# The preparation of the first scan segment, moved from behind the two opening fronts into the plan that holds them

## The chip, the cores and the metric

The kernel runs on one core of a Trainium2 chip, in one launch. The metric is the device time in microseconds (us). The engines named below are PE (matrix engine), DVE (vector), ACT (activations), POOL and SP; SP issues nearly all DMAs, in the order of its own queue. Every engine works its instructions off in program order, so the order in which the program is written out decides what can run beside what.

## The reference, cut to what matters

The input is a batch of 4 images of 64 x 64 tokens with 96 channels. Four layers follow one another. Layers 0 and 1 are state space layers: group norm, an input projection to 192 channels plus a gate z, a 3 x 3 depthwise convolution with SiLU, then a recurrence over the 4096 tokens in four directions, each with a state of 16 per channel:

```
h = h * exp(dt * A) + (dt * u) * B_t        # per channel and state
y = sum over states of h * C_t
```

`dt`, `B` and `C` are projections of the convolved tokens, taken in the order of the direction (in layer 0 two diagonal orders and two radial ones). The four results are summed in token order, normed, gated with z and projected. Layers 2 and 3 (attention, a Fourier mixer and feed-forward parts) come after the scans and are not touched here.

## The kernel before

`Stream.run` handles eight batches, four images for each of the two scan layers. Each batch has 4 directions of 4 segments of 1024 tokens, so 128 segments. Every batch passes three stages.

- **Front** (`front`, L348): four strips of 16 image rows are loaded (`measure` L368 the strip into a tile `da`, `edges` L380 its neighbour rows `halo`). DVE takes statistics (L372, L388), two tiny matmuls average them over groups (L391, L400), ACT takes the square root (L66). Then each strip is projected (`project`: L428 and L434 for x, L444, L447 and the store L452 for the gate) and convolved on PE (`convolve`: L481 the taps, L493 SiLU, L502 and L505 back to token rows, L514 the store to `x_tok` in DRAM).
- **Preparation** of a segment (`fetch` L736, `prepare` L779). The tokens are gathered from `x_tok` in scan order: for a diagonal direction one small DMA for each diagonal run (L745), 52 of them for the first segment. PE transposes them (L791), ACT puts them in order (L804), PE projects (L830), ACT and POOL form a softplus (L834, L835, L839, L818 to L822, L856), PE adds its three terms (L862), ACT copies `dt` (L867), POOL multiplies `dt` by x (L866, L876). B and C go to DRAM (L841), `dt` too (L869). They come back broadcast over partitions: B and C by `load_states` (L883, eight DMAs of 512 KB), `dt` by `load_dt` (L889).
- **Scan**: for 6 channel blocks and 4 state groups, PE spreads u (L898), ACT takes `exp` of the decays (L906), DVE multiplies by B (L911) and scans (L918), POOL multiplies by C (L928), PE sums over states (L939). In the middle of the kernel a segment's preparation is woven into the scan of the segment before it.

The fronts are put out by `side_by_side` (L686). It makes generators, called threads, and a `Plan` writes them out in the order of an estimated start on their engine: a thread yields an engine and a guess of the time, or a condition to wait for. Tiles in a `Rings` are marked taken and free while the program is written; a front that wants the PSUM bank `m` (one buffer) waits until its flag is free. Where the plan finds PE unoccupied it writes small spare matmuls (`fill`, L705).

The first call of `side_by_side` puts out the fronts of the first two batches; the second of them starts when every strip of the first is projected (`first.to_project == 0`). After that call, `run` writes the first segment's preparation alone, one step after the other, and then its eight B and C loads and the first `dt` load:

```python
self.side_by_side(batches[:2])
self.fetch(segs[0])
self.run_hooks(len(self.hooks), len(self.runs))
weave.start(self.prepare(segs[0]))
weave.finish()
```

`prepare` also counts in `self.put` how much PE time it has put out; `keep_busy` (L955) writes spare matmuls (L962) into the scan while that count is low.

Of the kernel before, what the change touches and what calls it, by code (L numbers as in the profile page):

```python
# [21 lines left out]
B = 4  # L22
HW = 64
L = HW * HW
# [4 lines left out]
SEG = 1024  # L29
# [8 lines left out]
NSG = NS // GS  # L38
# [162 lines left out]
class Rings:  # L201
# [9 lines left out]
    def take(self, pool, shape, tag, bufs, dtype=F32):  # L211
        ring = self.rings.setdefault(tag, SimpleNamespace(busy=[False] * bufs, at=0, tiles=None))
        while ring.busy[ring.at]:
            yield lambda: not ring.busy[ring.at]
        slot, ring.at = ring.at, (ring.at + 1) % bufs
        ring.busy[slot] = True
        x = ring.tiles[slot] if ring.tiles else self.k.t(pool, shape, tag, dtype, bufs=bufs)
        self.slots[id(x)] = ring, slot, x
        return x

    def give(self, *xs):
        for x in xs:
            ring, slot, _ = self.slots.pop(id(x))
            ring.busy[slot] = False
# [87 lines left out]
class Stream:  # L312
# [38 lines left out]
    def front(self, bt, plan, rings, first=None):  # L351

        k, nc, lay = self.k, self.nc, bt.lay
        take, give = rings.take, rings.give
        if first:
            yield lambda: first.to_project == 0
        bt.to_project = L // SEG
        x = lay.x_in[:, bt.b, :]
        bt.x_tok = k.t(self.dram, [L, DI], "x_tok", bufs=3)
        bt.z_t = k.t(self.dram, [C, 2, L], "z_t", bufs=3)  # L360
# [104 lines left out]
        def convolve(s, st):  # L465
            yield lambda: st.pad is not None
            xc = []
            for _ in range(C // GC):
                xc.append((yield from take(self.tmp, [128, CH], "xc", 3)))

            two = yield from take(self.ps_t, [128, 2, CH], "t", 2)
            one = yield from take(self.ps, [128, CH], "m", 1)
            ps = [two[:, 0, :], two[:, 1, :], one]
            yield "PE", 8.0
            for tap in range(9):
                dy, dx = divmod(tap, 3)
                for blk in range(C // GC):
                    mine = slice(blk * GC, (blk + 1) * GC)
                    for at in range(4):
                        half, j = divmod(at, 2)  # L480
                        nc.tensor.matmul(  # L481
                            ps[blk][at * GC : (at + 1) * GC, :],
                            lay.diag[mine, half, tap, :],
                            st.pad[mine, half, j * 8 + dy : j * 8 + dy + 8, dx : dx + HW],
                            start=tap == 0,
                            stop=tap == 8,
                            tile_position=(blk * GC, at * GC),
                        )
            give(st.whole)
            del st.whole, st.pad  # L490
            for blk in range(C // GC):
                yield "ACT", 0.7
                nc.scalar.activation(xc[blk], ps[blk], AF.Silu, bias=lay.conv_b[:, blk : blk + 1])  # L493
            give(two, one)
            del two, one, ps
            rows = yield from take(self.tmp, [128, 2, 4, DI], "y_rows", 1)
            two = yield from take(self.ps_t, [128, 2, CH], "t", 2)
            one = yield from take(self.ps, [128, CH], "m", 1)
            for blk, ps in enumerate((two[:, 0, :], two[:, 1, :], one)):
                yield "PE", 1.2  # L500
                for t in range(4):
                    nc.tensor.transpose(ps[:, t * 128 : (t + 1) * 128], xc[blk][:, t::4], k.ident)  # L502
                yield "ACT", 0.8
                for half in range(2):
                    nc.scalar.copy(  # L505
                        rows[:, :, :, half * C + blk * GC : half * C + (blk + 1) * GC],
                        ps.rearrange("p (t h j d) -> p h j t d", h=2, j=2, d=GC)[:, half],
                    )
            give(two, one, *xc)
            del two, one, ps, xc  # L510

            to = bt.x_tok[s * SEG : (s + 1) * SEG, :].rearrange("(j p t) d -> p j (t d)", j=2, t=4)
            yield "SP", 0.1
            nc.sync.dma_start(to, rows.rearrange("p j t d -> p j (t d)"))  # L514
            yield "none", 2.5
            give(rows)
            del rows

        works = [work for s, st in enumerate(strips) for work in (project(s, st), convolve(s, st))]
        yield from plan.together(works)  # L520

# [164 lines left out]
    def side_by_side(self, ahead, behind=None, flush=None, seg=None):  # L686


        k, nc = self.k, self.nc
        plan, rings = Plan(), Rings(k)  # L690
        self.ended, self.idle = False, None

        def ending():

            yield "none", 1.2
            if flush:
                flush()
            self.idle = k.t(self.ps_y, [128, CH], "y")
            self.ended = True
            yield "PE", 4.0  # L700

        def fill():
            if self.idle is not None:
                data = self.layers[0].diag.rearrange("p h t c -> p (h t c)")[:, :384]
                nc.tensor.matmul(self.idle[:GC, :384], self.zeros, data, start=True, stop=True)  # L705

        def states():

            for at in range(2 * NSG):
                yield "none", 50.0 if at == 0 else 4.0  # L710
                yield "SP", 0.1
                self.load_states(seg, *divmod(at, NSG))
            self.load_dt(seg, 0)

        plan.fill = fill
        if seg:
            plan.add(states())
        if behind:
            plan.add(self.merge(behind, plan, rings))
        for bt in ahead:  # L720
            plan.add(self.front(bt, plan, rings, None if bt is ahead[0] else ahead[0]), 1)
        plan.add(ending())
        plan.run()
        self.idle = None
# [11 lines left out]
    def fetch(self, seg):  # L736
# [11 lines left out]
        if seg.bt.lay.ordered and seg.kd < 2:  # L748

            for j in range(SEG // 128):  # L750
                at = seg.i * SEG + j * 128
                seg.turned[j] = []
                for pos, n, token, step in diagonal_runs(seg.kd, at, at + 128):
                    self.runs.append(lambda to=g[pos - at : pos - at + n, j, :], r=(token, n, step): run(to, *r))
                    seg.turned[j].append((pos - at, n, step < 0))
        elif seg.bt.lay.ordered:
            for j in range(SEG // 128):
                at = seg.i * (SEG // 128) + j
                self.hooks.append(
                    lambda j=j, at=at: nc.gpsimd.indirect_dma_start(  # L760
                        out=g[:, j, :],
                        out_offset=None,
                        in_=x_tok,
                        in_offset=bass.IndirectOffsetOnAxis(ap=self.order[:, seg.kd, at : at + 1], axis=0),
                    )
                )
        elif seg.kd % 2 == 0:
            at = self.start(seg)
            nc.sync.dma_start(g, x_tok[at : at + SEG, :].rearrange("(j p) d -> p j d", p=128))
        else:  # L770
            for w in range(2):
                nc.sync.dma_start(g[w * HW : (w + 1) * HW], self.by_columns(x_tok, seg, w))
# [238 lines left out]
    def run(self):  # L1011
# [1 line left out]


        k, nc, weave = self.k, self.nc, self.weave
        batches = [SimpleNamespace(lay=lay, b=b, to_project=1) for lay in self.layers for b in range(B)]
        segs = []
        for bt in batches:
            for kd in range(ND):
# [5 lines left out]
        slots = [(seg, cb, sg) for seg in segs for cb in range(NCB) for sg in range(0, NSG, 2)]  # L1025
        first_of = lambda slot: (slot[0].kd, slot[0].i, slot[1], slot[2]) == (0, 0, 0, 0)
        with k.tc.manual_schedule():
            self.side_by_side(batches[:2])
            self.fetch(segs[0])
            self.run_hooks(len(self.hooks), len(self.runs))  # L1030
            weave.start(self.prepare(segs[0]))
            weave.finish()
            for which in range(2):
                for sg in range(NSG):
                    self.load_states(segs[0], which, sg)
            self.load_dt(segs[0], 0)
            now, before = [], []

            def flush():
# [1071 lines left out]
```

## Time and profile before

| | us |
|---|---|
| median of 3 runs | 15879.18 |
| lowest and highest of the 3 runs | 15832.05 and 15962.23 |
| the profiled execution's own time | 15861.73 |
| its span in the profile | 15859.9 |
| first scan instruction (L918) starts at | 400.95 |
| last decay of the scans (L906) starts at | 12645.2 |

Over the whole span PE is busy 86%, DVE 81%, ACT 52% and POOL 62%; the mean granted PE clock of the execution is 0.875. Times inside the profile count from the start of the span. A row of a timeline gives start and duration, the engine, the line, the operation and its tiles, how many instructions are merged in it, and in brackets how long the engine was idle ahead of it and what ended that. SPq is SP's queue: its rows are the issuing of DMAs, not their transfer.

### The profile page before, as it was taken

To read this page: it belongs to the slowest core of one execution; us is meant where nothing else is said; L and a number is where in the kernel's file an instruction comes from. 1 tells how busy PE (TensorE), PEld (TensorE's weight loads), DVE (VectorE), ACT (ScalarE), POOL (GpSimd) and SP (SyncE) were. 2 spreads that over 40 slices of the span, in tenths; PEclk is the share of its full clock that TensorE was granted. 3 is DMA by queue.
4 is the path that set the end of the run, shared out by engine and by line. 5 is a ranking of instruction groups with operands and counts; after the bars stand their busy time and mean duration, and the time that the engine had idled before them with its cause. 6 is when DMAs were issued, how large, how long until landed. Compare 5 with 4: busy or idle time off the path is not lost. (4 is left out here: it accounts for less than half of the span.)

```text
span 15859.9 us, 190275 instructions
## 1 busy us (share of the span) xinstructions
PE 13616.6 (86%) x70721; PEld 4897.8 (31%) x70721; DVE 12867.0 (81%) x9642; ACT 8291.1 (52%) x14188; POOL 9781.6 (62%) x4913
## 2 busy tenths in 40 slices
PE   7888888888888888888888888888888889998877
PEld 3222322232223222322222223222222234443344
DVE  1989798979897989799979997999899965665555
ACT  3656465556565655556655655656556522332333
POOL 0788688867886788677757775777677730000223
PEclk8888888888898888888888888888888899998888
DMA  2333433343334333433343334333433310000132
GB/s 71 110 103 121 153 108 104 120 152 106 104 122 153 106 103 120 154 109 115 113 150 118 108 118 147 111 122 116 141 118 108 115 53 18 18 11 14 46 75 70
DMA packets 662747, 1637.10 MB, mean 103 GB/s; under 512 B 102822, under 2 KB 268459, under 8 KB 658044
## 3 DMA queue, kind: packets, MB, share of 16 engines
q1 hardware_dynamic: 624956, 1549.37, 30.9%
q0 software_dynamic: 36864, 75.55, 1.6%
q8 instruction: 560, 9.18, 0.2%
q14 instruction: 367, 3.01, 0.1%
HBM read 1295.03 MB, written 329.58 MB: 102 GB/s over the span
## 5 line engine op out<-in xcount | busy, mean ns | idle before, releaser
L928 POOL TENSOR_TENSOR hc<-h,bc 128x1024 f32<-128x1024 f32 x3072 | 7186.7, 2359 | 2360.7 <-DVE h L918 1949.8
L918 DVE TENSOR_TENSOR_SCAN h<-da,state,t 128x1024 f32<-128x1024 f32 x2304 | 5271.5, 2329 | 11.5 <-ACT da L906 8.7
L939 PE MATMUL y<-hc,gather_y 128*32 128x512 f32 x12288 | 4270.8, 687 | 628.4 <-POOL hc L928 465.1
L911 DVE TENSOR_TENSOR t<-u,bc 128x1024 f32<-128x1024 f32 x3072 | 3601.2, 1218 | 895.2 <-PE u L898 780.8
L906 ACT ACTIVATE da<-dts,L_A_logs 128x1024 f32<-128x1024 f32 x3072 | 3488.0, 1147 | 726.7 <-DMA dts<-dt_dram 444.4
L898 PE MATMUL u<-dtu,spread 32*128 32x512 f32 x3072 | 1879.7, 739 | 369.4 <-DVE t L911 362.9
L962 PE MATMUL y<-L_diag,zeros 96*32 96x256 f32 x5218 | 1736.9, 463 | 0.0
L918 DVE TENSOR_TENSOR_SCAN h<-da,t 128x1024 f32<-128x1024 f32 x768 | 1711.0, 2269 | 13.1 <-ACT da L906 12.5
L939 PEld LDWEIGHTS y<-hc,gather_y 128*32 128x32 f32 x12288 | 800.1, 117 | 2404.0 <-issue 1210.4
L830 PE MATMUL m<-xs,proj 96*128 96x512 f32 (+1 forms) x2048 | 1018.3, 620 | 121.8 <-ACT dt L839 62.7
L867 ACT COPY dt<-m 96x512 f32<-96x512 f32 x512 | 297.1, 580 | 1458.9 <-PE m L862 1458.9
L898 PEld LDWEIGHTS u<-dtu,spread 32*128 32x128 f32 x3072 | 595.1, 214 | 1433.1 <-issue 1117.5
L962 PEld LDWEIGHTS y<-L_diag,zeros 96*32 96x32 f32 x5218 | 617.2, 132 | 1274.9 <-issue 1114.7
L1289 POOL MEMSET padp<- 128x2448 f32 x32 | 68.6, 2143 | 1396.7 <-PE d L1329 1375.5
L1365 DVE SCALAR_TENSOR_TENSOR hcv<-padv,taps,hcv 128x2048 f32<-128x2048 f32 x384 | 902.2, 2350 | 13.4
L1329 PE MATMUL d<-padp,diag 32*32 32x512 f32 x25600 | 885.5, 601 | 2.0 <-ACT hcp L1344 2.0
L822 POOL TENSOR_TENSOR dtu<-sp_z,dtu 96x1024 f32<-96x1024 f32 x256 | 604.4, 2361 | 384.7 <-ACT dtu L820 382.3
L862 PE MATMUL m<-sp_z,ident 96*96 96x512 f32 x1024 | 537.1, 606 | 195.6 <-ACT sp_z L856 195.6
L834 ACT ACTIVATE sp_z<-m,L_dtb 96x512 f32<-96x512 f32 x512 | 349.3, 682 | 540.4 <-PE m L830 531.6
L1329 PEld LDWEIGHTS d<-padp,diag 32*32 32x32 f32 x25600 | 483.4, 103 | 370.6 <-issue 197.7
L986 ACT COPY spare<-m 128x512 f32<-128x512 f32 x384 | 225.6, 587 | 711.0 <-PE m L983 710.8
L830 PEld LDWEIGHTS m<-xs,proj 96*128 96x128 f32 (+1 forms) x2048 | 322.4, 177 | 829.4 <-issue 325.8
(275 smaller groups left out, 15623.6 us busy)
## 6 DMA issues: line engine op xcount, KB each, us to landing
bc<-bc_dram SPq DMA_DIRECT2D x1024, 512.0 KB
dts<-dt_dram SPq DMA_DIRECT2D x768, 512.0 KB
dt_dram<-dt SPq DMA_DIRECT2D x256, 384.0 KB
y_tok<-spare SPq DMA_DIRECT2D x64, 768.0 KB
dt<-y_tok SPq DMA_DIRECT2D x128, 384.0 KB
x_tok<-y_rows SPq DMA_DIRECT2D x32, 768.0 KB
z_t<-z_rows SPq DMA_DIRECT2D x64, 384.0 KB
dx<-x_tok SPq DMA_DIRECT2D x64, 384.0 KB
```

Of the source, the lines that this page charges most:

```text
L822: rest = lambda half: nc.gpsimd.tensor_add(r[:, half], z[:, half], r[:, half])
L830: nc.tensor.matmul(ps, proj[:, src, to], xs[:, src, cols], start=src == 0, stop=src == 1)
L862: nc.tensor.matmul(ps, k.ident[:C, :C], term[:, half, cols], start=at == 0, stop=at == 2)
L898: self.nc.tensor.matmul(seg.u[:, cols], self.spread[rows, :], seg.dtu[rows, half, cols], start=True, stop=True)
L906: self.nc.scalar.activation(da, seg.dts[cb], AF.Exp, scale=seg.bt.lay.neg_a[:, seg.kd, g : g + 1])
L911: self.nc.vector.tensor_mul(gr.t, gr.seg.u, self.bc[:, 0, gr.sg, :])
L918: self.nc.vector.tensor_tensor_scan(gr.h[:, order], gr.da[:, order], gr.t[:, order], start, op0=ALU.mult, op1=ALU.add)
L928: self.nc.gpsimd.tensor_mul(gr.hc, gr.h, self.bc[:, 1, gr.sg, :])
L939: nc.tensor.matmul(seg.y[at : at + GC, :], self.gather_y, gr.hc[:, part * CH : (part + 1) * CH], start=gr.sg == 0, stop=gr.sg == NSG - 1, ...
L962: self.nc.tensor.matmul(gr.seg.y[at : at + GC, :256], self.zeros, gr.seg.bt.lay.diag.rearrange("p h t c -> p (h t c)")[:, :256], start=Fal ...
L1329: nc.tensor.matmul(pc[i][j * 32 : (j + 1) * 32, :], diag[mine, ON_PE.index(t), tap, :], pad[mine, j * 8 + dy : j * 8 + dy + 8, dx : dx + H ...
L1365: nc.vector.scalar_tensor_tensor(to, win, wt, to, op0=ALU.mult, op1=ALU.add)
```

## The change

A thread `begin` joins the first call of `side_by_side`. It waits until the first batch has put out all its four stores of `x_tok` (the new counter `to_store`), writes the gathers, then steps through `prepare`, and at the end writes the eight loads of B and C and the first load of `dt`. While it steps it marks the bank `m` as taken. Afterwards it sets `self.put` to zero. The serial block in `run` goes.

```diff
-        bt.to_project = L // SEG
+        bt.to_project = bt.to_store = L // SEG
...
             nc.sync.dma_start(to, rows.rearrange("p j t d -> p j (t d)"))
+            bt.to_store -= 1
...
+        def begin(rings):
+
+            yield lambda: ahead[0].to_store == 0
+            self.fetch(seg)
+            self.run_hooks(len(self.hooks), len(self.runs))
+            yield "none", 6.0
+            work = self.prepare(seg)
+            bank = rings.rings["m"].busy
+            going = True
+            while going:
+                while bank[0]:
+                    yield lambda: not bank[0]
+                bank[0] = True
+                yield "PE", 1.0
+                put = self.put
+                going = next(work, self) is not self
+                while going and self.put > put:
+
+                    put = self.put
+                    yield "ACT", 1.4
+                    going = next(work, self) is not self
+                bank[0] = False
+            self.put = 0.0
+            for which in range(2):
+                for sg in range(NSG):
+                    self.load_states(seg, which, sg)
+            self.load_dt(seg, 0)
+
...
         if seg:
-            plan.add(states())
+            plan.add(states() if behind else begin(rings))
...
-            self.side_by_side(batches[:2])
-            self.fetch(segs[0])
-            self.run_hooks(len(self.hooks), len(self.runs))
-            weave.start(self.prepare(segs[0]))
-            weave.finish()
-            for which in range(2):
-                for sg in range(NSG):
-                    self.load_states(segs[0], which, sg)
-            self.load_dt(segs[0], 0)
+            self.side_by_side(batches[:2], seg=segs[0])
```

More of the change, by code (lines that the diff above doesn't have):

```diff
@@ L1015, in run @@
         k, nc, weave = self.k, self.nc, self.weave
-        batches = [SimpleNamespace(lay=lay, b=b, to_project=1) for lay in self.layers for b in range(B)]
+        batches = [SimpleNamespace(lay=lay, b=b, to_project=1, to_store=1) for lay in self.layers for b in range(B)]
         segs = []
```

## The prediction

> **What bounds the kernel now.** The change touches one place, the opening before the first scan, so I took the page's totals first, to see what the place is worth, and then asked the trace only about the opening.
>
> ```profile
> span 15859.9 us, 190275 instructions
> PE 13616.6 (86%) x70721; PEld 4897.8 (31%) x70721; DVE 12867.0 (81%) x9642; ACT 8291.1 (52%) x14188; POOL 9781.6 (62%) x4913
> DVE  1989798979897989799979997999899965665555
> POOL 0788688867886788677757775777677730000223
> ```
>
> Each digit is a slice of 396.5 us. The first has DVE at 1 and POOL at 0, the second DVE at 9 and POOL at 7: the scans begin with the second slice. Whatever makes the first scan start earlier shortens the kernel one for one, if nothing after it changes, and not more than the 401 us of the opening can be moved. I then cut the opening, by the timeline, where one stage hands over to the next, and asked for the stretches (start and end, their length, then busy us of each engine with counts, granted PE clock, DMA share, GB/s).
>
> ```profile
> 205.23:221.52 16.29, 9.63 (x29) 3.10 (x28) 5.40 (x9) 3.32 (x3) 0.00 (x0) 0.91 0.68 198
> 221.52:312.27 90.75, 85.87 (x1022) 41.86 (x1022) 5.06 (x18) 33.58 (x58) 0.00 (x0) 0.96 0.19 65
> 312.27:312.89 0.62, 0.00 (x0) 0.00 (x0) 0.00 (x0) 0.00 (x0) 0.00 (x0) 1.00 0.96 248
> 312.89:383.61 70.72, 37.28 (x58) 11.26 (x59) 0.00 (x0) 24.71 (x76) 7.02 (x3) 0.57 0.10 28
> 383.61:400.95 17.34, 1.29 (x4) 0.22 (x2) 2.46 (x2) 2.46 (x4) 2.34 (x1) 0.56 0.86 305
> ```
>
> Row 1 runs from the first batch's last `x_tok` store to the second front's first group-norm matmul: loads and statistics. Row 2 is that front's body, bound by PE (85.87 of 90.75). Row 4 is the preparation: no engine is much over half busy, it is a chain of hand-overs. Row 5 waits for the broadcast loads. The sum is 195.72 us, and every row is serial to the next. The timeline shows the hand-overs:
>
> ```profile
> 211.21 1.82 SPq L368 DMA_DIRECT2D da<-in_x  x4
> 221.44 0.45 PE L391 MATMUL m<-gn_mv,gavg 96*96 96x1 f32 x2 [6.66 <-DVE gn_mv L388]
> 312.89 20.00 SPq L745 DMA_DIRECT2D x_got<-x_tok  x52
> 350.25 3.73 PE L830 MATMUL m<-xs,proj 96*96 96x512 f32 x4 [2.04 <-ACT dt L839]
> 376.69 1.10 PE L862 MATMUL m<-dt,ident 96*96 96x512 f32 x2 [0.67 <-ACT dt L867]
> 384.03 5.41 SPq L883 DMA_DIRECT2D bc<-bc_dram  x8
> 389.49 0.65 SPq L889 DMA_DIRECT2D dts<-dt_dram  x1
> 399.78 3.23 ACT L906 ACTIVATE da<-dts,L_A_logs 128x1024 f32<-128x1024 f32 x3 [14.87 <-DMA dts<-dt_dram]
> 400.95 4.46 DVE L918 TENSOR_TENSOR_SCAN h<-da,t 128x1024 f32<-128x1024 f32 x2 [9.17 <-ACT da L906]
> 407.58 4.46 DVE L918 TENSOR_TENSOR_SCAN h<-da,t 128x1024 f32<-128x1024 f32 x2
> 418.88 4.46 DVE L918 TENSOR_TENSOR_SCAN h<-da,t 128x1024 f32<-128x1024 f32 x2 [0.30 <-ACT state L924]
> ```
>
> The first scan waits for a decay, the decay 14.87 us for the `dt` load, and that stands in SP's queue behind eight loads of 512 KB. Between the second and third pair of scans 11.3 us pass instead of 6.6.
>
> **What the skill says.** The Trainium skill, "TensorE: Matmul & The Clock Gate", section "What's actually happening", has PE at half clock after an idle window of some 3.4 us and at full clock after a busy one. The trace agrees in kind: four L830 matmul pieces take 3.73 us at 350.25 and 1.96 at 431.03, and the granted clock is 0.50 from 338 to 361 and 1.00 from 376 to 384. But PE stayed at half clock through 23 us in which it was 65% busy, so a busy window needs more than that. "DMA: Bandwidth & Descriptors", section "Two DMAs through the same engine are not ordered", has the issuing engine wait on a DMA's semaphore before it issues one that reads its result. So SP must stand still until `dt` has landed in DRAM before it can load it back, and holds whatever is queued behind. The trace shows the load issued at 389.49 after the stores had been issued from 376.66 on.
>
> **The change part by part.** Built, both kernels have 9644 DVE, 14190 ACT, 4918 POOL and 4706 SP instructions; PE has 19 matmuls more, 16 spare ones of L962 and 3 of L705. From the second front's end on the order is the same on all engines, L962 apart. In between, PE and ACT of the new kernel have the whole preparation ahead of the second front's first matmul L391, in one block; nothing is interleaved. The cause is in the thread: at the end of a step it frees the bank `m` and takes it again within the same call, so the second front, waiting for that flag, never sees it free. The preparation comes *before* the second front, not beside it. What runs beside it is only what needs no bank: the front's DMA loads and DVE statistics.
>
> Gathers. SP now issues the 52 of them straight after the fourth `x_tok` store, at 205.25. They pass the last two gate stores, three halo and four strip loads of the second front. The loads come 20 us later, at about 230, their statistics (5.4 us of DVE) near 245, while the bank is held to about 271: hidden. The uncovered 16.29 us of row 1 go, and so do the 0.62 us of row 3.
>
> Preparation. 70.72 us as before, less what a warm PE saves. Each piece is now followed by a spare matmul (0.64 us warm, 1.28 cold by halving the clock), placed in the wait for ACT. A cycle of 5.82 us (344.43 to 350.25) that was 3.78 busy becomes 5.06 busy, 87%, as dense as the one that turned warm at 376.69 (5.16 of 5.79). Upper bound of the saving: three L830 groups 1.8 each and two L862 groups 1.7 and 2.3, together 9.4; lower bound 0, if the idle stretch before the logarithm (PE 363 to 366.5) and the gather phase keep it cold. Spare matmuls could also stretch the hand-overs by a few tenths. I take 5: 65.7 us, to 270.95.
>
> The second front's body then runs its 90.75 us, to 361.7. Its ACT square root needs its table anew, 1.28 us, but ACT comes free when PE starts the group-norm pair, 2.3 us (221.44 to 223.75) before the root is due: nothing.
>
> Loads back. The eight of B and C, the `dt` load, and before them one projection load and three stores to DRAM, 65 DMAs with the gathers, are all issued before the second front's first `x_tok` store, at 251.32 - 221.52 + 271 = 301. SP is held to about 277 and DMA to about 288 (4.7 MB at the 418 GB/s of this place): no front DMA waits. Row 5's 17.34 us go. What is late next is PE: the last L444 ends 1.1 us before ACT's last gate tile, then u takes 1.98 and two L911 1.23 each; ACT needs a table (1.28) and a decay (1.15) and is ready earlier. First scan 3.6 us after the body, at 365.3.
>
> Sum: 16.29 + 0.62 + 17.34 - 3.6 + 5 = 35.65 us earlier than 400.95.
>
> First segment after that. The second segment's 27 gathers still stand ahead of the second `dt` load in SP's queue. Before, they took 21.18 us beside the broadcast loads, started 10.4 us ahead of the first scan, and ended 10.8 us after it. Now they follow the last gate store, about 364.5; at the first gathers' 0.385 each they take 10.4 and end 9.6 us after the first scan. So the stalls of 4.7 and 5.1 us (scans 407.58 to 418.88, 425.51 to 437.21) stay about the same. Bound: 10 us gained if both vanish, 10 lost if the gathers are as slow as before. The 16 spare matmuls, 0.46 us each or twice that cold, lie in PE's gaps; at worst 15 us of PE, of which I count a few. Together I take 0.
>
> So 15861.7 - 35.6 = 15826 on the profiled execution's own time. That execution lay 17.5 us below the median of the three runs; on the median, 15879.2 - 35.6 = 15844 us.
>
> **The rivals**, each on the median. *Cold and crowded*: PE stays at half clock in the preparation and the second segment's gathers cost 10: 35.6 - 5 - 10 = 20 gained, 15859. For it: 0.54 clock in the gather phase; against it the 87%. *Stalls vanish too*: 35.6 + 9.8 = 45, 15834; for it that the broadcast loads no longer share the DMA engines, against it that the gathers start later against the scan. *Truly beside*: PE's sum decides, 16.3 + 90.75 + about 19 (37.28 at half clock) + 3.6 = 129.6 in place of 195.7, 66 gained, 15813; the built order speaks against it. *Slower*: the second front follows a preparation with PE half idle and, not warming, runs at half clock; its 85.87 busy us double, 35.6 - 85.9 = 50 lost, 15929. It decides once more than 36 us of the front's PE work are cold. Against it: before, the front began at 0.91 and was back at 1.00 within 40 us, at 95% busy.
>
> **How the numbers follow.** Forecast 0.70, cold 0.17, stalls vanish 0.08, truly beside 0.02, slower 0.03. The first three give 15834 to 15859. The runs shown lie 130 us apart for one and the same program, more than the effect; a median of such runs can be off by some 50. So 15780 to 15910. A measurement of this kernel tells from no change what is over 1% (159 us). No case reaches that; only the scatter leaves something: faster 0.03, same 0.95, slower 0.02.
>
> **What would show it.** Right: L391 of the second front after the last L867 copy; no wait for `bc` or `dts` ahead of the first scan; that scan at 358 to 372; from it to the end 15459 as before, within the scatter. Wrong: a first scan after 380 (cold PE, or SP held), gathers seen between the front's convolutions, or a longer distance from the first scan to the last decay (12244 us now).

## The result, and the profile after

| | before | after |
|---|---|---|
| median, us | 15923.51 (20 runs, 15832.05 to 15970.63) | 15880.03 (20 runs, 15818.63 to 15956.00) |
| ratio, 95% interval | | 0.9976 [0.9963, 0.9988] |
| profiled execution, us | 15861.73 | 15876.61 |
| first batch's last `x_tok` store | 204.84 | 205.78 |
| first scan | 400.95 | 382.60 |
| distance of the two | 196.1 | 176.8 |

In this measurement the changed kernel is a quarter of a per cent faster. The forecast had 15844 us as a time, on a median of 15879 for the kernel before, which is a ratio of 0.9978. The ratio came out; the time did not come out as closely, because the kernel before itself measured 15924 with more runs. And the place that the gain was to come from did not deliver it: the opening became 19.3 us shorter, not 35.6. Timed again beside the experiments below, the same changed kernel came to 15864.62 (14 runs) against 15884.88 (52 runs), 0.9989 [0.9975, 1.0003], and that is what 19 us are worth: 1 - 19/15885 = 0.9988. The first measurement probably holds some luck on top.

The page of the kernel after, the same four lines as for the kernel before (the insertion shifts line numbers: L830 of the kernel before is L859 here, L862 is L891, L918 is L947; in the experiments they are a few higher again):

```profile
span 15874.8 us, 190347 instructions
PE 13637.9 (86%) x70759; PEld 4902.6 (31%) x70759; DVE 12868.4 (81%) x9642; ACT 8292.0 (52%) x14188; POOL 9781.0 (62%) x4913
DVE  1989798979897989799979997999899965665555
POOL 0888688868886888677757775777677720000223
```

The busy totals and the slices hardly differ, so the page says no more than that nothing large moved. (This one execution lies 15 us above the one of before, while the medians lie the other way: one profiled time decides nothing here, and I compare stretches inside the profiles.) The opening of the kernel after, cut where its stages hand over; columns are start and end, length, busy us of PE, PE's weight loads, DVE, ACT and POOL with their counts, granted PE clock, DMA share, GB/s:

```profile
206.22:239.60 33.38, 15.03 (x36) 3.85 (x35) 4.34 (x7) 7.24 (x54) 0.00 (x0) 0.60 0.45 126
239.60:263.00 23.40, 21.61 (x26) 5.37 (x26) 1.16 (x3) 11.77 (x16) 2.14 (x1) 0.50 0.02 6
263.00:278.00 15.00, 11.53 (x15) 2.80 (x14) 0.00 (x0) 6.04 (x7) 2.55 (x2) 0.51 0.00 0
278.00:285.60 7.60, 7.60 (x18) 2.07 (x16) 0.00 (x0) 1.73 (x4) 2.34 (x1) 1.00 0.18 54
285.60:379.43 93.83, 87.68 (x1024) 42.92 (x1024) 6.76 (x18) 34.84 (x59) 2.33 (x1) 0.95 0.33 117
379.43:382.60 3.17, 0.80 (x2) 0.00 (x0) 2.27 (x3) 3.14 (x3) 0.00 (x0) 1.00 0.71 210
```

Rows 1 to 4 are the preparation, 79.4 us in all where 65.7 was forecast; row 5 is the second front's body, row 6 the way to the first scan. Both serial waits of the kernel before are gone: no row of loads and statistics ahead of the preparation, none for the broadcast loads behind it. But the preparation itself grew. The timeline of after shows where:

```profile
206.22 20.14 SPq L774 DMA_DIRECT2D x_got<-x_tok  x52
226.45 1.23 SPq L452 DMA_DIRECT2D z_t<-z_rows  x2
227.81 2.81 SPq L380 DMA_DIRECT2D halo<-in_x  x3
230.98 1.72 SPq L368 DMA_DIRECT2D da<-in_x  x4
232.75 0.42 SPq L814 DMA_DIRECT2D proj<-L_proj  x1
239.60 3.75 PE L859 MATMUL m<-xs,proj 96*128 96x512 f32 x4 [7.24 <-DMA proj<-L_proj]
278.61 1.10 PE L891 MATMUL m<-dt,ident 96*96 96x512 f32 x2
285.63 0.33 PE L391 MATMUL m<-gn_mv,gavg 96*96 96x1 f32 x2
382.60 4.46 DVE L947 TENSOR_TENSOR_SCAN h<-da,t 128x1024 f32<-128x1024 f32 x2
399.60 2.36 DVE L940 TENSOR_TENSOR t<-u,bc 128x1024 f32<-128x1024 f32 x2 [5.93 <-PE u L927]
401.00 1.15 ACT L935 ACTIVATE da<-dts,L_A_logs 128x1024 f32<-128x1024 f32 x1 [9.90 <-DMA dts<-dt_dram]
402.32 4.46 DVE L947 TENSOR_TENSOR_SCAN h<-da,t 128x1024 f32<-128x1024 f32 x2 [0.36 <-ACT state L953]
```

Row 6 is the surprise. The first projection of the preparation (L859) waits 7.24 us for its weights. Their load stands in SP's queue behind nine DMAs of the two fronts (the first front's last two gate stores, the second's seven loads), which come after the gathers now and did not stand there before. The other rows answer to the forecast: L391 follows the last `dt` copy at once (285.55 and 285.63), and the first scan waits for neither `bc` nor `dts`. The last three rows are the stall between the second and third pair of scans, as before: 19.7 us from first to third pair (17.9 before).

### The profile page after: what moved, and what is told of

Its sections match the earlier page's. It is cut to its first block, busy times and chain, and to the rows that moved or that the text cites. A ratio compares the mean times of both kernels' runs of the same rounds, so it can differ in the third digit from the quotient of the medians.

```text
span 15874.8 us, 190347 instructions
## 1 busy us (share of the span) xinstructions
PE 13637.9 (86%) x70759; PEld 4902.6 (31%) x70759; DVE 12868.4 (81%) x9642; ACT 8292.0 (52%) x14188; POOL 9781.0 (62%) x4913
## 5 line engine op out<-in xcount | busy, mean ns | idle before, releaser
L947 DVE TENSOR_TENSOR_SCAN h<-da,state,t 128x1024 f32<-128x1024 f32 x2304 | 5271.5, 2329 | 16.4 <-ACT da L935 14.4
L947 DVE TENSOR_TENSOR_SCAN h<-da,t 128x1024 f32<-128x1024 f32 x768 | 1711.4, 2269 | 9.6 <-ACT da L935 9.0
L859 PE MATMUL m<-xs,proj 96*128 96x512 f32 (+1 forms) x2048 | 1017.2, 619 | 119.1 <-ACT dt L868 58.1
L891 PE MATMUL m<-sp_z,ident 96*96 96x512 f32 x1024 | 536.2, 605 | 189.5 <-ACT sp_z L885 189.5
L859 PEld LDWEIGHTS m<-xs,proj 96*128 96x128 f32 (+1 forms) x2048 | 321.9, 177 | 826.5 <-issue 335.5
```

Of the source, the lines that this page charges most:

```text
L859: nc.tensor.matmul(ps, proj[:, src, to], xs[:, src, cols], start=src == 0, stop=src == 1)
L891: nc.tensor.matmul(ps, k.ident[:C, :C], term[:, half, cols], start=at == 0, stop=at == 2)
L947: self.nc.vector.tensor_tensor_scan(gr.h[:, order], gr.da[:, order], gr.t[:, order], start, op0=ALU.mult, op1=ALU.add)
```

## The experiments

The measure is D, the distance from the first batch's last `x_tok` store to the first scan: 196.1 before, 176.8 after. The first four are single executions, read by D; the others were timed. The four ran on another chip than the timed ones; the kernel before took 15998 us there, once, and its opening was not profiled there. Two profiles of the changed kernel gave 176.8 and 178.2, so nothing is read into a us or two.

**Weights ahead of the gathers.** Theory: the wait for the weights is what is missing.

```diff
             yield lambda: ahead[0].to_store == 0
+            self.load_proj(seg)
...
             self.fetch(seg)
...
```

> The changed kernel with one edit: the load of the projection weights is issued ahead of the 52 gathers of the first segment, instead of behind them and behind the nine DMAs of the two fronts. Measured by D, the distance from the first batch's last x_tok store to the first scan: 196.1 us in the kernel before, 176.8 in the kernel after. Theory (SP's queue order held the weights back): the first projection matmul waits no longer for the weights, D falls by 7 to 8, to about 169. Rival (the wait lay beside another one, the transposes or a cold PE decide): D stays at 175 to 178.

The wait went, and the projection began 27.6 us after the `x_tok` store instead of 33.8. Yet D was 177.8, no better than 176.8. The timeline of this kernel:

```profile
207.94 0.39 SPq L514 DMA_DIRECT2D x_tok<-y_rows  x1
235.57 3.78 PE L867 MATMUL m<-xs,proj 96*128 96x512 f32 x4
282.11 2.02 PE L899 MATMUL m<-dt,ident 96*96 96x512 f32 x2
287.41 0.33 PE L391 MATMUL m<-gn_mv,gavg 96*96 96x1 f32 x2
```

The last group of L899 still takes 2.02 us for two matmuls, where the kernel after has 1.10: PE stayed at half clock to 285.7, which is 77.8 us after the `x_tok` store; in the kernel after it was 71.9 (277.7). From one group to the next the last two took 6.8 us (275.33 to 282.11) and 5.3 (to 287.41) instead of 3.5 each. These 5.1 us took back most of the 6.2 that the early start had gained: L391 came 79.5 us after the `x_tok` store, instead of 79.9. So the weights' wait is real, but in this opening removing it alone gained nothing: when PE turns to full clock decides too.

**The bank flag seen free.** One line lets the plan's other threads see the bank between two steps; the rest is the changed kernel.

```diff
                 bank[0] = False
+                yield "none", 0.0
```

> The changed kernel with one edit: after each step the thread gives the bank m back and lets the plan turn to another thread before it takes it again. Theory (the bank flag alone kept the second front behind the preparation, and PE's order now mixes both, but the front in its turn keeps the bank and the last four product groups L891 fall behind it): D about 172, between 165 and 180; the broadcast loads are waited for again at the end. Rival (once freed, the two truly run side by side): D 130 to 140.

The second front's L391 now comes at 245.36, ahead of the first projection, so the flag was what made the preparation one block. But D is 180.8, 4.0 more than with the block. At the start PE waits 14.45 us for the front's statistics. Then preparation and front take turns at one bank, the preparation falls behind, and its end comes after the front's:

```profile
245.36 0.45 PE L391 MATMUL m<-gn_mv,gavg 96*96 96x1 f32 x2 [14.45 <-DVE gn_mv L388]
379.06 1.23 DVE L941 TENSOR_TENSOR t<-u,bc 128x1024 f32<-128x1024 f32 x1 [77.80 <-DMA bc<-bc_dram]
389.74 3.23 ACT L936 ACTIVATE da<-dts,L_A_logs 128x1024 f32<-128x1024 f32 x3 [14.87 <-DMA dts<-dt_dram]
390.92 4.46 DVE L948 TENSOR_TENSOR_SCAN h<-da,t 128x1024 f32<-128x1024 f32 x2 [9.19 <-ACT da L936]
```

So the waits that the block had covered, for the front's statistics and for `bc` and `dts`, are both back. And the late end of the preparation is at half clock again: from 349.5 to 377.0 PE is busy 27.50 of 27.50 us at a granted clock of 0.50.

**The block alone between the fronts.** The kernel before, with the serial block of `run` moved between two calls of `side_by_side`, one for each batch; no thread.

```diff
-            self.side_by_side(batches[:2])
+            self.side_by_side(batches[:1])
             self.fetch(segs[0])
             ...
             self.load_dt(segs[0], 0)
+            self.side_by_side(batches[1:2])
```

> The kernel before with the serial preparation block placed between the two fronts, each put out by a call of its own; no thread. Theory (moving the block only hides the broadcast loads, 17 us; the second front's loads and statistics, 16 us, are covered in the changed kernel because they are issued from the same plan, and here they stand behind the broadcast loads): D about 191. Rival (the order of the block is all that counts): D about 177 or less.

D was 198.1, where 191 was expected: nothing gained. The stretch from the broadcast loads' issue to L391, in this kernel, and its rows in SP's queue:

```profile
283.00:308.00 25.00, 1.32 (x5) 0.22 (x2) 5.39 (x9) 0.54 (x1) 1.73 (x1) 0.60 0.84 270
```

```profile
282.68 6.07 SPq L883 DMA_DIRECT2D bc<-bc_dram  x8
288.79 0.66 SPq L889 DMA_DIRECT2D dts<-dt_dram  x1
293.67 4.26 SPq L368 DMA_DIRECT2D da<-in_x  x4
308.16 0.45 PE L391 MATMUL m<-gn_mv,gavg 96*96 96x1 f32 x2 [23.84 <-DVE gn_mv L388]
```

For 25 us the engines do next to nothing (PE 1.32 us, DVE 5.39) while DMA is 84% busy: the front's loads queue behind 4 MB of broadcasts. The order "preparation, then front" alone hides the broadcasts and uncovers the loads. The gain of the changed kernel comes from the plan's having put the front's loads and statistics ahead of the preparation's matmuls.

**More spare matmuls.** The forecast had argued that a denser PE turns warm sooner. Each matmul step of the preparation gets one spare matmul more.

```diff
                 going = next(work, self) is not self
+                if self.put > put:
+                    fill()
```

> The changed kernel with one more spare matmul of 384 columns after every matmul step of the first preparation. Theory (PE works through the preparation at half clock because it idles in each hand-over; filled up, it turns to full clock): granted clock near 1.00 in the projection groups, four of them 3.75 to 2.0 us, D down by 5 to 9, to about 169. Rival (clock stays at 0.5, or the hand-overs to ACT decide): D 177 to 182.

D was 179.9. The window in the middle of the preparation:

```profile
239.00:265.00 26.00, 26.00 (x33) 6.39 (x33) 0.76 (x2) 13.00 (x17) 2.34 (x1) 0.50 0.02 5
```

PE is busy for 26.00 of 26.00 us, as the profile reckons it (it models the ends of matmuls), and the granted clock is 0.50 throughout; it turned full at 279.3. So more spare matmuls did not bring the full clock. They multiply by zero weights (`zeros`), so one could ask whether they count as work; but in the 27.5 us of the one-line experiment above most matmuls were the preparation's own, and the clock stayed at 0.50 there too.

**The changed kernel again, and with the second segment's gathers early.** The 27 gathers of the second segment are issued directly after the first `dt` load, from 293.94, instead of after the last gate store.

```diff
             self.load_dt(seg, 0)
+            self.run_hooks(len(self.hooks), len(self.runs))
```

> The changed kernel itself, timed again beside the kernel before. Theory (the whole gain lies ahead of the first scan: D, the distance from the first batch's last x_tok store to the first scan, 196.1 to 176.8): ratio 0.9988, within 0.998 and 1.000; D 177 again; the scans take as long as before but for their scatter. Rival (as much again is gained later in the scans): ratio 0.9976 or less, and the stretch from the first scan to the last one shorter by some 20 us.

> The changed kernel with one edit: the 27 gathers of the second segment are issued at the end of the thread, behind the first dt load, instead of at the start of the scans. Theory (in the first segment PE and the second dt load wait for these gathers): D stays near 177, but the third pair of scans starts 13.3 us after the first pair instead of 19.7, and the later stall shrinks; together 8 to 11 us, ratio about 0.9982. Rival (the stall is ACT's and PE's order, half clock): the third pair stays at 18 to 20 us, ratio as of the changed kernel.

D was 178.2 and 176.1. The third pair of scans came 19.3 us after the first in the one, 13.7 in the other; the ratios were 0.9989 [0.9975, 1.0003] and 0.9985 [0.9973, 0.9998]. So the gathers' place behind the front was what kept the stall alive, and moving them takes 5.6 us of it.

**Truly beside.** The thread puts its products in the bank of `u`, which is idle before the first scan, and takes no flag; the front's loads go ahead of the gathers; PE's turn goes to the thread first. Two of the thread's guesses of time change as well (6.0 to 10.0, 1.4 to 0.7), and the cut shows one of three places where the bank is chosen.

```diff
-            yield lambda: ahead[0].to_store == 0
+            yield lambda: ahead[0].to_store == 0 and ahead[0].to_project == 0
+            yield "none", 3.0
+            yield "none", 0.0
...
-                while bank[0]:
-                    yield lambda: not bank[0]
-                bank[0] = True
...
-            plan.add(states() if behind else begin(rings))
+            plan.add(states() if behind else begin(rings), None if behind else 2)
...
-            ps = k.t(self.ps, [C, 2, 256], "m")
+            ps = self.bank([C, 2, 256])
```

> The changed kernel, with its thread made to run truly beside the second front: its products go into the PSUM bank u, which is idle in the opening, so that no flag is shared; the second front's loads are issued ahead of the gathers; the thread has precedence. Theory (the bank alone made it a block; what is left is bound by PE: the front's 86 us and the preparation's 19 at full clock): D 138, between 130 and 155, ratio about 0.9965. Rival (PE takes its orders one by one, and the preparation's hand-overs to ACT, POOL and the gathers now stop the front's products too): D 155 to 172, ratio 0.998.

D was 148.6, 28 us less than the changed kernel, ratio 0.9979 [0.9968, 0.9989]. What each of these edits gave by itself was not measured. From the `x_tok` store at 207.30 to the first scan at 355.89, PE is busy 124.03 of 148.59 us at a mean clock of 0.86: here PE's own work sets most of the time.

**Beside, with the early gathers.** The last version with the one line of the early gathers.

> Both edits together: the thread truly beside the second front, and the second segment's gathers issued at its end. Theory: the gains add up, D as in the kernel with the first of the two alone (138), the third pair of scans 13.3 us after the first, ratio about 0.996, the fastest of all. Rival: 27 gathers in SP's queue hold back the front's remaining stores and neighbour rows, D 5 to 15 longer than with the first edit alone, and nothing is won by adding the second.

The two do not add up: D was 163.1, 14.5 worse; the third pair came 13.2 us after the first, 5.8 better; ratio 0.9981 [0.9968, 0.9995]. The timeline of this kernel:

```profile
331.13 21.25 SPq L774 DMA_DIRECT2D x_got<-x_tok  x27
352.47 0.38 SPq L514 DMA_DIRECT2D x_tok<-y_rows  x1
359.59 1.02 ACT L447 ACTIVATE z_rows<-t 96x1024 f32<-96x1024 f32 x1 [18.37 <-DMA z_t<-z_rows]
361.20 1.13 PE L502 MATMUL t<-ident,xc 128*128 128x128 f32 x4 [18.08 <-ACT y_rows L505]
```

and the same places without the early gathers:

```profile
331.25 0.38 SPq L514 DMA_DIRECT2D x_tok<-y_rows  x1
344.60 1.02 ACT L447 ACTIVATE z_rows<-t 96x1024 f32<-96x1024 f32 x1 [3.88 <-DMA z_t<-z_rows]
346.20 0.80 PE L502 MATMUL t<-ident,xc 128*128 128x128 f32 x4 [3.59 <-ACT y_rows L505]
```

Read it from the top. The gathers hold SP for 21.25 us beside the broadcasts; the front's gate and `x_tok` stores stand behind them; ACT finds no free gate tile for 18.37 us, and PE waits 18.08 for ACT. With the block of the changed kernel the same gathers (19.88 us from 293.94) ended ahead of the front's first store at 319, and cost nothing.

**Beside, gathers spread.** Instead of at once, they go out in threes in the plan, between the front's own DMAs.

```diff
-            self.run_hooks(len(self.hooks), len(self.runs))
+            while self.runs:
+                yield "none", 2.4
+                yield "SP", 0.1
+                self.run_hooks(0, 3)
```

> The thread beside the front, with its products in the idle accumulator bank, and the 27 early transfers of the next chunk put out in groups of three between the front's own transfers, instead of all at once. Theory (the early transfers cost the front only because they stood in one block ahead of its stores): the first scan comes 149 us after the first batch's last x_tok store (145 to 155), as without them, the third pair of scans 13.3 us after the first instead of 19, and the ratio is about 0.9972. Rival (any transfer in SP's queue ahead of the front's stores delays the front by its issue time): 155 to 163 us, and no gain over the version without early transfers (0.998).

```profile
205.36 0.39 SPq L514 DMA_DIRECT2D x_tok<-y_rows  x1
331.07 4.23 SPq L777 DMA_DIRECT2D x_got<-x_tok  x3
336.41 0.76 SPq L452 DMA_DIRECT2D z_t<-z_rows  x1
337.60 7.84 SPq L777 DMA_DIRECT2D x_got<-x_tok  x12
354.78 4.45 DVE L958 TENSOR_TENSOR_SCAN h<-da,t 128x1024 f32<-128x1024 f32 x2
368.02 4.45 DVE L958 TENSOR_TENSOR_SCAN h<-da,t 128x1024 f32<-128x1024 f32 x2
```

Both gains are there: D 149.4, third pair 13.2 us after the first, ratio 0.9976 [0.9964, 0.9989]. Up to the seventh pair of scans it is the shortest of all; its ratio can't be told apart from that of the version without the early gathers.

The timed versions side by side. "Seventh pair" is the distance from the `x_tok` store to the seventh pair of scans, past the stalls; the next column is what that distance alone would give, 1 - (245.6 - distance)/15885:

| | D | seventh pair | from it | measured ratio |
|---|---|---|---|---|
| before | 196.1 | 245.6 | | |
| after | 176.8 | 228.8 | 0.9989 | 0.9976 [0.9963, 0.9988] |
| after, again | 178.2 | 230.7 | 0.9991 | 0.9989 [0.9975, 1.0003] |
| gathers early | 176.1 | 219.2 | 0.9983 | 0.9985 [0.9973, 0.9998] |
| beside | 148.6 | 200.4 | 0.9972 | 0.9979 [0.9968, 0.9989] |
| beside, gathers early | 163.1 | 203.3 | 0.9973 | 0.9981 [0.9968, 0.9995] |
| beside, spread | 149.4 | 191.7 | 0.9966 | 0.9976 [0.9964, 0.9989] |

All but the first line of the changed kernel lie inside their intervals, and that misses by 0.0001. So these versions gain in the opening and nowhere else that these measurements show. The three versions "beside" measured a smaller gain than their distance would give, all three by some 11 to 16 us; whether a part is lost again later, the intervals are too wide to say. None comes near a per cent: 54 us is the most that any of them took out of the opening.

## Why the prediction was right or wrong

**What failed, in short.** The sum for the opening: 35.65 us forecast, 19.3 found. Three of its terms were wrong. The step on the gathers put at nothing what stands behind them in SP's queue, and the first projection, waiting there for its weights, came 7.7 us late. The warm PE in the preparation was taken as 5 us and gave -0.95. The second front's body was taken as unchanged and was 3.1 longer. The forecast's own sign of being wrong came: the first scan at 382.60, after 380 and not within 358 to 372, and with both causes named there (a cold PE, a load held in SP's queue).

**What held.** The profile's first reading stood: the opening is serial to the scans, and only it moves. The block order was right, with the reason given for it (the flag; shown by the one-line experiment). The 16.29 and 17.34 us rows did go, and the first scan waits for neither broadcast. "The stalls stay about the same" was right: 19.7 us to the third pair against 17.9. From the first scan to the last decay nothing was gained: 12272 and 12269 us in the two profiles of the changed kernel, 12244 before. A longer distance was another sign of being wrong; but the other timed versions spread from 12199 to 12288, so one profile can't tell a loss of 28 us from scatter. "No case reaches 1%" was right, and the time lay inside the range.

**Gathers: the step that failed first.** It listed what the 52 gathers pass, "the last two gate stores, three halo and four strip loads", and asked only who waits for *those*. It did not ask who stands behind them in turn. The preparation's own weights load did: it left 26.5 us after the gathers began (206.22 to 232.75), and L859 started 33.4 us after them, 7.7 us late. In the kernel before the same load left 20.1 us after the gathers (312.89), and the projection started after 25.7 without waiting for it:

```profile
332.94 0.31 SPq L785 DMA_DIRECT2D proj<-L_proj  x1
338.61 3.78 PE L830 MATMUL m<-xs,proj 96*128 96x512 f32 x4 [1.09 <-ACT xs L804]
```

The later count, "65 DMAs with the gathers ... no front DMA waits", looked from the front's side only, too.

**Preparation: the warm PE.** I took 5 us off for it, between bounds of 0 and 9.4. From the first projection to the last `dt` copy the kernel after took 45.95 us, before 45.0: the value was -0.95, just outside the bounds, and the step was 5.95 off. The argument ("a cycle ... 87%, as dense as the one that turned warm") is refuted: 100% for 26 us did not turn it warm. The spare matmuls filled waits and gave nothing here. The kernel before was at half clock from 314.1 to 375.6, the one after from 212.9 to 277.7: some 62 and 65 us, whatever the density. The Trainium skill, "TensorE: Matmul & The Clock Gate", section "What's actually happening", has full clock after one busy window of about 3.4 us. As a sufficient condition the trace contradicts that (26.00 and 27.50 us busy at 0.50), and the measurement decides. In the second front's body the full clock did come, but later than after 3.4 us: after some 7.4 us of unbroken PE work in the kernel before (221.4 to 228.8) and 9.9 in the kernel after (288.35 to 298.2). What does turn the clock is not settled here: with the weights early it turned 5.9 us later after the `x_tok` store, though PE had started earlier.

**The second front's body.** Taken as 90.75, it was 93.83, 3.1 longer. Some 1.7 of it is L396, 1.86 us where it took 0.15 before. It ran beside the preparation's last product on POOL; first the row of the kernel before, then two of the kernel after:

```profile
222.12 0.15 DVE L396 TENSOR_TENSOR gn_d<-gn_mv,gn 96x1 f32<-96x1 f32 x1
286.18 1.86 DVE L396 TENSOR_TENSOR gn_d<-gn_mv,gn 96x1 f32<-96x1 f32 x1
285.70 2.33 POOL L905 TENSOR_TENSOR dtu<-dt,xs 96x1024 f32<-96x1024 f32 x1 [4.67 <-ACT dt L896]
```

In the kernel after, L396 ends at 288.04, the product at 288.03. With the weights early the two ends are 289.82 and 289.82 (287.96 + 1.86, 287.48 + 2.34), with more spare matmuls 291.18 and 291.17 (289.96 + 1.22, 288.83 + 2.34); where no POOL product runs beside it, L396 takes 0.15. The Trainium skill, "SBUF — State Buffer", section "SBUF: two separate sides", has DVE and POOL share one pair of ports, and a DVE operation with two SBUF inputs wait for a POOL operation that reads SBUF for the whole of that. The trace agrees in every one of these cases. The forecast had the front follow the block and did not look at what the block leaves running. The rest is read, not tested: of the body's PE work 9.9 us were at half clock (to 298.2), before 7.4; 2.5 us more at half speed cost about 1.2, an estimate from these two. The scan followed 3.17 us after the body instead of 3.6.

The sum: 7.7 + 5.95 + 3.1 - 0.4 = 16.3, and 35.65 - 16.3 = 19.3, as measured. That is where the us went; it is not what each cause is worth, since the terms aren't independent: taking the first away alone gave nothing.

**The rivals.** *Cold and crowded* named the size, 20 us, and half the reason: PE did stay cold. Its other half, gathers that cost 10, was 1.8; the weights load and the body, which it did not have, made up the sum. I had called it refuted by "the 87%", and gave it 0.17. *Truly beside*, worked out at 129.6 us, was built: 148.6. It was a better kernel, not what the change did. The *slower* one had a place (a cold front) and a trace of truth: 10 us of it at half clock, not the 36 that decide.

**The whole.** 15844 was forecast on a median of 15879 from three runs; the same kernel before measured 15924 with twenty. The forecast ratio, 0.9978, agreed with 0.9976 most likely by luck: the scatter of the first measurement added about what the opening lacked; timed again it was 0.9989. A matching total is no proof of the steps: the trace is.

## What to carry to other kernels

When a block of DMAs is moved in a queue, go through the moved step's own later DMAs as well: what it passes now stands ahead of them, weights loads too. A thread that frees and takes a resource within one call never yields it, so the plan makes a block of it; here its own idle buffer, with the front's loads first and its own turn ahead, did better than a share of the front's. Spread long runs of small DMAs between the stores that they would hold. When the forecast saving is under the scatter of a run, compare distances between two events inside the profiles: here D came within 1.4 us in two profiles of one kernel, where single runs scattered by tens.

## What the runs showed of the hardware

PE stayed at half clock through 26.00 and 27.50 us of fp32 matmuls without a gap in the profile, and for 61 to 68 us in each opening with the preparation serial; I had expected a dense stretch to end it. In the second front it ended after 7.4 us of unbroken work in the kernel before, and after 9.9 and 12.6 in the two profiles of the kernel after. The 27 gathers took 14.44 to 15.03 us to issue late in the opening and 19.88 to 21.25 right behind the broadcast loads. A DVE subtraction of one element in each of 96 partitions took 1.86 us instead of 0.15 when it started beside a POOL product of 2.33 us, and ended with it.
